# Registers from SBUF, one queue for the early weights, one table load and later mixes at the head of a conditional FFN kernel

## The chip, the cores and the metric

The kernel runs on one core of one Trainium2 chip. The metric is the device time of one execution in microseconds (us). Before the change the median of three runs is 1345.63 us (1345.31 to 1346.24). Differences of about 0.2%, some 2.7 us, are at the edge of what can be measured here.

## What is computed

The reference, cut to what matters:

```python
W = weights[condition]                       # (64, 64, 64), condition: 64 numbers from 0 to 15
y = einsum('bct,bcd->bdt', x, W)             # x as (64, 64, 1024)
y = y.reshape(4, 512, 1024)                  # read as the FFN's input
h = gelu(einsum('bsd,df->bsf', y, inter_w) + inter_b, approximate=True)   # F = 4096
out = x + einsum('bsf,fd->bsd', h, output_w) + output_b
```

x is (32, 64, 1024) in the inputs: 32 items with 64 channels and 1024 columns, so `condition` (called `cond` in the kernel) has 32 numbers that are used, and the result has the shape of x. All is float32. The first line matters most for this change: each item of x is multiplied by one of 16 matrices of 64 x 64, and which one is known only when the program runs.

## The kernel before

**Mixes.** Two items of x make a tile of 128 rows, so there are 16 tiles x_0 to x_15 (`NR` is 16). A *mix* (`mix`, from L299) multiplies one tile with a block-diagonal matrix of 128 x 128, `wsel(i)`, whose two blocks of 64 x 64 are the two items' matrices. It is eight matmuls into two PSUM tiles, and as float32 each is two instructions, 16 in all. The off-diagonal blocks are zeroed once by VectorE (`zero_wsel`). The diagonal blocks are fetched by `load_wsel` (from L263), two DMAs of 16 KB a tile, from `cond_w` at an address in a register; `load_indices` (from L251) reads eight such registers at a time, those of four tiles. The tiles 0 to 7 have their own blocks in `wsel_e`, the tiles 8 to 15 share two in `wsel_l` (`NL` is 8).

Mixes 0 to 7 (`mixed`, from L311) fill the first half of y in SBUF: ScalarE copies one PSUM tile, VectorE the other. Mixes 8 to 15 are for the second half: `load_later` brings tile and weights, `mixed_later` copies out, `store_later` writes to DRAM, where it is read again later. The order of the first eight is 0, 1, 2, 3, 6, 7, 4, 5.

**Products.** The two large products of the FFN are done by a scheme of Strassen's kind in two levels, 7 x 7 products of blocks where 8 x 8 would be needed. In its place come sums of blocks. POOL (GpSimd) makes those of the weights (`inner_w1`, `outer_w1`, through `pool_add`). VectorE and ScalarE make those of y and of the hidden values: `to_psum` copies one operand to PSUM (ScalarE, L202, tile t) and `add` sums on VectorE (L182). `right_sums` strings four such sums together. A product (`mm1`, L500) has eight instructions; it adds into one of the PSUM banks A, B and C, and `read` adds the bank into its target (fX, fD, ...) on VectorE, or copies it on ScalarE where the target is new (L475). w11, w12, w21 and w22 are the four blocks of the first piece of `inter_w`, 1 MB each.

**Order.** Every step is entered by hand with a due time, `at(time, fn, ...)`, and `run` sorts the steps by time and calls them. Times are in units of one product, 0 at the start of the first block; a block (`plan_block`) has seven products and begins every 7 units. Each engine does its instructions in that order, and waits in place for what they need. So do the two queues that issue DMAs: SP, which issues nearly all, and ScalarE, which issues some between its copies. The framework gives each DMA one of eight semaphores in turn, and an issue waits until the DMA before it on the same semaphore has landed.

**The head.** In the order of due times: `warm` (from L280) multiplies zeros, 11 times, while nothing has arrived; registers and weights of tiles 0 to 3 are read and issued on ScalarE, directly from `cond` in DRAM; the registers of tiles 4 to 7 are read on SP, also from DRAM, between the issue of x_1 and that of x_2; the weights of tiles 4 to 7 are issued on SP between the loads of x. `cond_s` is a copy of `cond` in SBUF, from which the later registers are read. Mixes 0, 1 and 2 come ahead of the first two products (fA, fB), then mixes 3, 6, 7, 4, 5, then the rest of block 0. Mixes 8 to 15 have the due times in `later` (L684). The first two of them use banks of the products, B and C; the others use the two PSUM buffers through which ScalarE's copies t also go (`pst`).

The activation table that ScalarE needs for a function is loaded ahead of the first instruction that needs another one than is loaded: before the change once ahead of the first copy and once ahead of the first gelu.

Of the kernel before, what the change touches and what calls it, by code (L numbers as in the profile page):

```python
# [9 lines left out]
F32 = mybir.dt.float32  # L10
AF = mybir.ActivationFunctionType
# [63 lines left out]
def kernel(  # L75
# [35 lines left out]
    nc = tc.nc  # L111
    P = 128
    B, C, T = x.shape
    S, _, D = cond_w.shape
    F = inter_w.shape[1]
    assert 2 * C == P and 2 * D == P
    NR = B // 2
# [31 lines left out]
    NL = 8  # L149
    b1 = const.tile([P, F // P], F32, name="b1")  # L150
    wsel_l = const.tile([P, 2, P], F32, name="wsel_l")
    cond_s = const.tile([1, B], cond.dtype, name="cond_s")
# [3 lines left out]
    misc = left1.enter_context(tc.tile_pool(name="misc", bufs=2))  # L156
# [16 lines left out]
    def at(time, fn, *args):  # L173
        steps.append((time, len(steps), fn, args))
# [30 lines left out]
    def right_sums(time, get, gap=0.5):  # L205


        e = {}
        v = nc.vector

        def one():
            e.update(get())
            e["p"] = to_psum(e["12"])

        def two():
            add(v, e["t3"], e["22"], e["p"], sub=True)

        def three():
            add(v, e["t1"], e["p"], e["11"], sub=True)
            e["p"] = to_psum(e["11"])  # L220

        def four():
            add(v, e["t2"], e["p"], e["t3"])
            e["p"] = to_psum(e["21"])

        def five():
            add(v, e["t4"], e["p"], e["t2"], sub=True)

        for j, f in enumerate((one, two, three, four, five)):
            at(time + j * gap, f)  # L230
# [11 lines left out]
    def wsel(i):  # L242
        return wsel_e[:, i, :] if i < NR - NL else wsel_l[:, i % 2, :]
# [7 lines left out]
    def load_indices(i0):  # L251


        eng = mybir.EngineType.SP if i0 else mybir.EngineType.Activation
        src = cond[None, :] if i0 < NR - NL else cond_s
        _, idx = nc.values_load_multi_w_load_instructions(
            src[:, 2 * i0 : 2 * i0 + 8], engines=[eng], min_val=0, max_val=S - 1,
            skip_runtime_bounds_check_because="the reference indexes cond_w by it",
        )
        for k, v in enumerate(idx):  # L260
            IDX[2 * i0 + k] = v

    def load_wsel(i):  # L263
        eng = nc.sync if i > 3 else nc.scalar
        for j in range(2):
            eng.dma_start(
                wsel(i)[j * C : (j + 1) * C, ts(j, D)],
                cond_w[bass.ds(IDX[2 * i + j], 1), :, :].rearrange("s c d -> (s c) d"),
            )
# [10 lines left out]
    def warm():  # L280


        z = misc.tile([P, 3 * P], F32, tag="m8", name="zeros")
        nc.vector.memset(z, 0.0)
        t = acc_pool.tile([P, 2, W], F32, tag="A", name="warm")
        for _ in range(11):
            nc.tensor.matmul(t[:, 1, :], z[:, :P], z[:, P:], start=True, stop=True)  # L287

    Y = {}
# [27 lines left out]
    def load_later(i):  # L317
        t = misc.tile([P, 2, T], F32, tag="m8", name=f"xl{i}")
        XT[i] = t[:, 0, :]
        YS[i] = t[:, 1, :].rearrange("p (k n) -> p k n", k=NK)  # L320
        nc.sync.dma_start(XT[i], x_rows[i])
        load_wsel(i)
# [50 lines left out]
    def inner_y(a, p):  # L373
        q = Y[a, RIGHT[p]]
        pool = yia if p in (1, 2) else late["yib"]
        t = lambda n: pool.tile([P, 2, W], F32, tag=f"yi{p}", name=f"y{n}_{a}_{p}")
        t1 = blk(q, 0, 1)
        if (a, p) == (0, 1):
            t1 = cpool.tile([P, 2, W], F32, tag="c", name="yi1_0_1")
        YI[a, p] = {  # L380
            "11": blk(q, 0, 0),
            "21": blk(q, 1, 0),
            "22": blk(q, 1, 1),
            "12": blk(q, 0, 1),
            "t1": t1,
            "t2": t("i2"),
            "t3": t("i3"),
            "t4": t("i4"),
        }
        return YI[a, p]  # L390
# [250 lines left out]


    at(-61, warm)
    order = FIRST
    at(-60.5, zero_wsel, wsel_e)
    at(-60, load_indices, 0)
    for i in range(4):
        at(-59, load_wsel, i)
    at(-50, load_indices, 4)
    for n in Y_ORDER:  # L650
        at(-45, new_y, 0, n)
    MIX = 1.06
    NB = 3
    t0 = 2 - (len(order) - NB) * MIX
    M_AT = {i: t0 + (j - NB) * MIX - (2 if j < NB else 0) for j, i in enumerate(order)}
    for j, i in enumerate(order):
        t = M_AT[i]
        if j < 6:
            at(-55 if j < 2 else -43 + 0.1 * j, load_x, i)
        else:  # L660
            at(M_AT[order[j - 6]] + MIX + 0.45, load_x, i)
        if i > 3:
            at(-43 + 0.1 * j, load_wsel, i)
        at(t, mix, i, None if j == 3 else "CB"[j % 2])
        at(t + MIX + 0.3, mixed, i)
    at(-54, lambda: nc.sync.dma_start(cond_s, cond[None, :]))
    t8 = M_AT[1] + MIX + 0.6
    at(-20, zero_wsel, wsel_l)
    at(t8, load_indices, 8)
    at(t8 + 0.5, load_indices, 12)  # L670
    at(-42.75, load_w1, 0, "11")
# [9 lines left out]
    right_sums(ty + 9.2, outer_y0(1, 0))  # L681
    for j, p in enumerate((6, 7, 4, 5, 3)):
        right_sums(7 * (j + 2) - (3.6 if p == 6 else 4.5), lambda p=p: inner_y(0, p))
    later = (4.02, 7.05, 12.5, 14.3, 21.8, 26.2, 33, 46.6)  # L684
    for j, t in enumerate(later):
        i = NR - NL + j
        at(max(t - 6, later[j - 2] + 3.3) if j > 1 else t8 + 0.4, load_later, i)
        at(t, mix, i, "BC"[j] if j < 2 else None)
        at(t + 1.4, mixed_later, i)
        at(t + 3.2, store_later, i)  # L690

# [8 lines left out]
    for it in range(nit):  # L700
# [5 lines left out]
        for n, t in W_AT.items():  # L706
            if it == 0:
                t = {1: -7.9, 2: -5.4, "s3": -4, "s1": -1}.get(n, t)
# [17 lines left out]
        if it == 1:  # L726
            for k in range(KQ):
                e = {}
                t = b0 + 5 + 10.8 * k
# [3 lines left out]
        elif it >= 2:  # L733
            n = -(-len(w2_pieces) // (nit - 2))
            for j in range(n):
                i = (it - 2) * n + j
                if i < len(w2_pieces):
                    e = {}
                    t = b0 + 9.5 + 14 * j
# [404 lines left out]
```

## Time and profile before

| what | value |
|---|---|
| median of three runs | 1345.63 us |
| the profiled execution: its own time | 1344.67 us |
| its span in the profile | 1342.7 us |
| TensorE (PE) busy | 1325.1 us, 99% |
| POOL, VectorE (DVE), ScalarE (ACT) busy | 945.6, 882.6, 486.5 us |
| mean granted TensorE clock | 0.999 |
| moved by DMA | 273.34 MB, mean 204 GB/s |

The span runs from the first to the last instruction that the profile records; the execution's own time is 2.0 us longer. Names like `py<-wsel_e,x` are the tile that is written and those that are read, with buffer numbers left out: `py` is a mix, `fA`, `fB` and `fC` are products by bank, `yi` and `yt` are sums of y, `wi` and `ws` sums of the weights, `xl` a late tile of x. "Idle before" is the time that an engine stood still ahead of an instruction, and behind the arrow stands what ended it.

Two things of the table can be misread. A busy PE is one that has an instruction in flight; at half clock it is as busy as at full. And the 70% of POOL and 66% of DVE are means over a kernel of several stages.

### The profile page before, as it was taken

How to read it: one execution, taken by the hardware profiler on the slowest of the kernel's cores; microseconds unless marked ns; L12 is line 12 of the kernel's file. 1: busy time of each engine (PE TensorE's matmuls, PEld its weight loads, DVE VectorE, ACT ScalarE, POOL GpSimd, SP SyncE). 2: the span in 40 equal slices, each digit the busy share in tenths (PEclk: the TensorE clock that was granted, in tenths of full speed). 3: DMA queues.
4: the chain of work that ended last, by engine and by line, in shares of the span. 5: the costliest groups of instructions: out<-in, count | busy, mean ns of one | idle time of the engine just before them, and what ended most of it. 6: DMA issues, size and time to landing. Idle time of an engine off the chain costs nothing.

```text
span 1342.7 us, 18524 instructions
## 1 busy us (share of the span) xinstructions
PE 1325.1 (99%) x6286; PEld 1163.0 (87%) x6286; DVE 882.6 (66%) x1573; ACT 486.5 (36%) x975; POOL 945.6 (70%) x583
## 2 busy tenths in 40 slices
PE   8899999999999999999999999999999999999998
PEld 7888888888888888888888888888888888888887
DVE  4667565575786765757658574675766757767776
ACT  3424324243353442534415332333324333333341
POOL 3754757948768396594962967949959599496793
PEclk9999999999999999999999999999999999999999
DMA  7656676777897866768749145183360723916712
GB/s 272 168 163 221 211 223 233 258 261 257 298 352 225 284 211 222 257 204 273 239 176 341 30 166 226 47 324 115 102 275 4 287 109 108 362 40 222 264 47 63
DMA packets 138176, 273.34 MB, mean 204 GB/s; under 512 B 17635, under 2 KB 71139, under 8 KB 126435
## 3 DMA queue, kind: packets, MB, share of 16 engines
q1 hardware_dynamic: 137170, 271.91, 58.8%
q8 instruction: 50, 0.82, 0.2%
q14 instruction: 44, 0.35, 0.1%
q10 hardware_dynamic: 912, 0.26, 0.1%
HBM read 167.27 MB, written 104.86 MB: 203 GB/s over the span
## 4 chain that ended last, share of the span: by engine, by line
PE 90%; DVE 4%; issue 2%; ACT 2%; POOL 1%; DMA 1%; SPq 0%; DVEq 0%; POOLq 0%; ACTq 0%
PE fA L500 26%; PE zA L511 24%; PE fC L500 12%; PE zC L511 12%; PE fB L500 7%; PE zB L511 6%; PE py L306 2%; DVE hs L182 1%; PE tp L998 1%; ACT t L202 1%; DMA wsel_l<-in_L_cond_weights_dram 1%; DVE fX L182 1%; POOL w2p L182 1%; PE warm L287 0%; DVE fV L182 0%
## 5 line engine op out<-in xcount | busy, mean ns | idle before, releaser
L500 PE MATMUL fA<-yi,wi 128*128 128x256 f32 x896 | 212.6, 380 | 3.3 <-DVE fX L182 1.5
L182 DVE TENSOR_TENSOR hs<-h,t 128x512 f32<-128x512 f32 x308 | 200.0, 679 | 5.6 <-ACT t L202 2.9
L511 PE MATMUL zA<-hs,wt 128*128 128x256 f32 x840 | 197.8, 379 | 0.0
L182 POOL TENSOR_TENSOR h<-h,h 128x1024 f32<-128x1024 f32 x84 | 196.1, 2364 | 0.0
L500 PEld LDWEIGHTS fA<-yi,wi 128*128 128x128 f32 x896 | 169.0, 190 | 29.8 <-issue 2.9
L511 PEld LDWEIGHTS zA<-hs,wt 128*128 128x128 f32 x840 | 158.5, 190 | 21.1
L182 POOL TENSOR_TENSOR wi<-w 128x512 f32<-128x512 f32 x80 | 101.7, 1272 | 53.0 <-PE fC L500 25.6
L525 ACT ACTIVATE fD<-fD,b 128x256 f32<-128x256 f32 x128 | 57.9, 500 | 186.2 <-DVE fD L182 181.7
L182 POOL TENSOR_TENSOR ws<-w,w 128x1024 f32<-128x1024 f32 x32 | 74.9, 2363 | 66.9 <-PE fA L500 47.5
L202 ACT COPY t<-h 128x512 f32<-128x512 f32 x140 | 81.8, 589 | 75.3 <-DVE hs L182 69.9
L202 ACT COPY t<-hs 128x512 f32<-128x512 f32 x112 | 65.4, 588 | 108.0 <-DVE hs L182 108.0
L182 POOL TENSOR_TENSOR wt<-v 128x512 f32<-128x512 f32 x35 | 44.6, 1274 | 82.5 <-DMA v<-w_d 70.2
L182 DVE TENSOR_TENSOR fX<-fA,fX 128x512 f32<-128x512 f32 x104 | 71.3, 685 | 44.4 <-PE fA L500 42.3
L182 POOL TENSOR_TENSOR wi<-w,wi 128x512 f32<-128x512 f32 x40 | 50.9, 1272 | 61.9 <-PE fA L500 48.7
L500 PE MATMUL fC<-y,wi 128*128 128x256 f32 x352 | 83.2, 379 | 0.1
L511 PE MATMUL zC<-hs,v 128*128 128x256 f32 x336 | 79.6, 379 | 0.8 <-DVE hs L182 0.8
L511 PE MATMUL zA<-h,wt 128*128 128x256 f32 x320 | 75.6, 379 | 0.0
L500 PE MATMUL fA<-yi,w 128*128 128x256 f32 x320 | 75.6, 379 | 0.0
L500 PEld LDWEIGHTS fC<-y,wi 128*128 128x128 f32 x352 | 66.7, 190 | 9.5 <-issue 0.5
L511 PEld LDWEIGHTS zC<-hs,v 128*128 128x128 f32 x336 | 63.6, 190 | 9.7 <-DVE hs L182 1.2
L500 PEld LDWEIGHTS fA<-yi,w 128*128 128x128 f32 x320 | 60.8, 190 | 8.3
L511 PEld LDWEIGHTS zA<-h,wt 128*128 128x128 f32 x320 | 60.6, 190 | 8.2
(181 smaller groups left out, 2778.1 us busy)
## 6 DMA issues: line engine op xcount, KB each, us to landing
h<-hs_d SPq DMA_DIRECT2D x56, 1024.0 KB, 5.3
w<-in_L_ffn_inter_w_dram SPq DMA_DIRECT2D x32, 1024.0 KB, 6.3
hs_d<-hs SPq DMA_DIRECT2D x96, 256.0 KB, 3.1
v<-w_d SPq DMA_DIRECT2D x21, 1024.0 KB, 9.8
hs_d<-fD SPq DMA_DIRECT2D x64, 256.0 KB, 3.4
w2p<-in_L_ffn_output_w_dram SPq DMA_DIRECT2D x32, 512.0 KB, 5.0
w_d<-w2p SPq DMA_DIRECT2D x64, 256.0 KB, 2.9
w_d<-w2t SPq DMA_DIRECT2D x48, 256.0 KB, 6.6
```

What stands on the lines that cost most here:

```text
L182: eng.tensor_tensor(o, a, b, ALU.subtract if sub else ALU.add)
L202: nc.scalar.copy(t, src)
L306: nc.tensor.matmul(PY[i][k // KQ][:, k % KQ, :], XT[i][:, ts(k, P)], wsel(i), start=True, stop=True,)
L500: nc.tensor.matmul(acc[:, u, :], lt[:, k, ts(u, P)], rt[:, k, :], start=start and u == 0 and k == 0, stop=k == 1, skip_group_check=True,)
L511: nc.tensor.matmul(acc, wl[:, k, :], hr[:, k, :], start=start and k == 0, stop=k == NG - 1, skip_group_check=True,)
L525: nc.scalar.activation(t[:, u, :], t[:, u, :], AF.Gelu_apprx_tanh, bias=b1[:, f : f + 1])
L998: nc.tensor.transpose(tp[:, v, ts(n0, P)], d[:, n0, ts(v, P)], late["ident"])
```

## The change

Six edits, all of them at the head:

- All registers are read from `cond_s` in SBUF, whose load becomes the first DMA that SP issues. Those of tiles 0 to 7 are read on ScalarE, the others on SP.
- ScalarE alone issues the weights of tiles 0 to 7. Those of 6, 7, 4 and 5 now stand behind the copies of mixes 0, 1 and 2.
- SP thereby has nothing to wait for between x_1, x_2 and w11.
- A gelu on one column of zeros is put ahead of everything on ScalarE, so that its table is loaded there. Copies need no table of their own behind it: the changed program has one table load, the old one two.
- Eight products of zeros instead of eleven.
- The late mixes 8 to 11 are due at 7.05, 11.03, 14.3 and 18.7 instead of 4.02, 7.05, 12.5 and 14.3. The first two change their banks. On TensorE that moves mix 8 behind three more products, mix 9 behind four, mix 10 behind two, mix 11 behind four; all else keeps its order.

```diff
     def load_indices(i0):
-        eng = mybir.EngineType.SP if i0 else mybir.EngineType.Activation
-        src = cond[None, :] if i0 < NR - NL else cond_s
+        eng = mybir.EngineType.SP if i0 >= NR - NL else mybir.EngineType.Activation
         _, idx = nc.values_load_multi_w_load_instructions(
-            src[:, 2 * i0 : 2 * i0 + 8], engines=[eng], min_val=0, max_val=S - 1,
+            cond_s[:, 2 * i0 : 2 * i0 + 8], engines=[eng], min_val=0, max_val=S - 1,
...
     def load_wsel(i):
-        eng = nc.sync if i > 3 else nc.scalar
+        eng = nc.sync if i >= NR - NL else nc.scalar
...
         t = acc_pool.tile([P, 2, W], F32, tag="A", name="warm")
-        for _ in range(11):
+        g = misc.tile([P, 1], F32, tag="m8", name="table")
+        nc.vector.memset(g, 0.0)
+        nc.scalar.activation(g, g, AF.Gelu_apprx_tanh)
+        for _ in range(8):
             nc.tensor.matmul(t[:, 1, :], z[:, :P], z[:, P:], start=True, stop=True)
...
     at(-60.5, zero_wsel, wsel_e)
+    at(-62, lambda: nc.sync.dma_start(cond_s, cond[None, :]))
     at(-60, load_indices, 0)
     for i in range(4):
         at(-59, load_wsel, i)
-    at(-50, load_indices, 4)
+    at(-58, load_indices, 4)
...
         if i > 3:
-            at(-43 + 0.1 * j, load_wsel, i)
+            at(M_AT[order[min(j - 4, 2)]] + MIX + 0.31, load_wsel, i)
...
-    at(-54, lambda: nc.sync.dma_start(cond_s, cond[None, :]))
...
-    later = (4.02, 7.05, 12.5, 14.3, 21.8, 26.2, 33, 46.6)
+    later = (7.05, 11.03, 14.3, 18.7, 21.8, 26.2, 33, 46.6)
     for j, t in enumerate(later):
...
-        at(t, mix, i, "BC"[j] if j < 2 else None)
+        at(t, mix, i, "CB"[j] if j < 2 else None)
```

## The prediction

> **What bounds the kernel now.** I read the page's busy line first, then PE's own waits, then the timeline and the clock of the stretch that the edits touch.
>
> ```profile
> span 1342.7 us, 18524 instructions
> ...
> PE 1325.1 (99%) x6286; PEld 1163.0 (87%) x6286; DVE 882.6 (66%) x1573; ACT 486.5 (36%) x975; POOL 945.6 (70%) x583
> ```
>
> PE bounds: only 17.6 us of the span is idle on it, and 8.8 of those lie in the first 90 us. PE's waits there (total, times, longest):
>
> ```profile
> PE py L306 <- DMA wsel_l<-in_L_cond_weights_dram: 4.0, 1, 4.0
> PE py L306 <- issue: 1.9, 1, 1.9
> PE py L306 <- DVE yi L182: 1.7, 1, 1.7
> PE warm L287 <- DVE zeros L284: 1.3, 1, 1.3
> ```
>
> All but the last stand in front of a mix (py; mix i works on x_i). The timeline places them (start, duration; ACTq and SPq are queues that issue DMAs):
>
> ```profile
> 4.51 5.17 ACTq L266 DMA_DIRECT2D wsel_e<-in_L_cond_weights_dram  x8
> 7.29 0.36 SPq L278 DMA_DIRECT2D x<-in_x_dram  x1
> ...
> 9.71 1.28 ACT L314 ACT_TABLE_LOAD   x1 [9.71 <-issue]
> ...
> 13.42 2.02 PE L306 MATMUL py<-wsel_e,x 128*128 128x128 f32 x16 [1.85 <-issue]
> ```
>
> Before 4.51 ACT reads its eight registers from cond in DRAM. SP does the same to 5.6 and then waits for the landing of wsel_e's second load at 7.28; only then may x_2 go. Mix 2 waits for its second half of weights, issued at 7.85 and landed 5.5 us later, 13.33. By start of instructions, mix 8 stands still from 31.22 to 35.38 (4.16) and mix 10 from 54.47 to 56.29 (1.82). The clock, in stretches (us, PE busy (count), granted clock, DMA share, GB/s):
>
> ```profile
> 35.38:38.86 3.48, 3.48 (x16) 0.51 0.93 16
> 56.29:58.18 1.89, 1.89 (x16) 1.00 0.69 269
> ```
>
> So mix 8 pays twice: its 16 instructions run at half clock and take 3.48 instead of the 16 x 0.111 = 1.78 of mixes 0 and 1.
>
> **Part by part.** Sums are against the profiled execution: 1344.67 us, of which 1342.7 is span and 2.0 lies around it. The runs' median, 1345.63, is 0.96 above; the forecast for a median adds that back.
>
> *Fewer zero products.* A product is two instructions. They start 0.43 apart until 4.81 and 0.216 apart from there. The six that go are among the later: 6 x 0.216 = 1.30. The last of 16 starts at 6.32, so mix 0 can start at 6.53 instead of 7.83, if its weights are there.
>
> *Registers from SBUF.* ACT's reads cost 0.88 + 2.71, SP's 2.51 + 0.92. From SBUF eight cost 0.53 to 0.71 (engine, instruction, count: ns min/median/max, first and last start).
>
> ```profile
> L256 SPq TENSOR_LOAD <-cond_s x2: 532/622/713, 22.8 to 28.6; - x2
> L256 ACTq TENSOR_LOAD <-in_itok_B_dram_ptr x1: 877/877/877, 0.7 to 0.7; - x1
> L256 ACTq TENSOR_LOAD <-in_itok_B_dram x1: 2712/2712/2712, 1.6 to 1.6; - x1
> L256 SPq TENSOR_LOAD <-in_itok_B_dram_ptr x1: 2512/2512/2512, 2.0 to 2.0; - x1
> ...
> L256 SPq TENSOR_LOAD <-in_itok_B_dram x1: 922/922/922, 4.7 to 4.7; - x1
> ```
>
> But now ACT waits for cond_s: issued at 0.74, landing about 2.0 later by the first wsel_e row below, 2.75. The read ends at 3.4, and the first wsel_e goes at 3.5 instead of 4.51, the second at 4.2. The table load (1.28 from 0.74, then a 1-column activation) ends by 2.4, inside that wait: cost nothing; if cond_s landed at once, up to 1.3.
>
> *SP is free early.* x_0, x_1, x_2 and w11 go from 1.1 to 2.4 instead of 0.74, 1.20, 7.29 and 7.71. So 2.5 MB are queued before the first wsel_e, and these rows (KB, issue to landing) decide the head:
>
> ```profile
> wsel_e<-in_L_cond_weights_dram ACTq DMA_DIRECT2D x4, 16.0 KB, 2.0
> ...
> wsel_e<-in_L_cond_weights_dram ACTq DMA_DIRECT2D x1, 16.0 KB, 6.4
> ```
>
> The four issued with little else under way took 2.0; those issued behind x_2, w11, x_3 and x_6 took 4.0, 5.5, 6.3 and 6.4. The last three landed 0.5 to 1.1 before the large load issued ahead of each did (w11 by POOL's first sum, 13.96). x_0 took 3.6 and x_1 came 1.25 after it, so x_0, x_1, x_2, w11 land at 4.7, 5.95, 7.2 and 9.7. I take 0.5 before w11: both halves for mix 0 at 9.2. Bounds: 6.53 (nothing in the way) and 4.2 + 6.4 = 10.6.
>
> Then mix 0 runs at 9.25, mix 1 at 11.0, mix 2 at 12.8, and the first product fA at 9.25 + 3 x 1.78 = 14.6 instead of 15.28: **-0.7**, from -3.4 (9.25 becomes 6.53, fA 11.9) to +2.3 (10.6, and mix 0 at half clock).
>
> The new list of waits ties queues together, since eight DMA semaphores go round and an issue waits until the one before on its semaphore has landed (before, SP stood 2.6 us so):
>
> ```profile
> SPq L278 <- DMA wsel_e<-in_L_cond_weights_dram: 2.6, 2, 1.7
> ```
>
> x_3 waits for mix 0's weights, x_6 for w11, x_7 for mix 1's. On ACT the copies of mixes 0 to 2 alternate with wsel_e 6, 7, 4, 5, at 0.65 a piece (5.17 / 8), and the last four of these wait for x_3, x_6 and x_7. By x_2's 3.7 and 1.3 more for each following, these land at 12.9, 14.2 and 15.5. The last wsel_e is out at 16.8, and the copy of fA runs to 17.4. Mix 7 needs the bank behind it and starts at 14.6 + 2 x 1.73 + 2 x 1.78 = 21.6 (1.73 for a product of eight instructions), so 3 us cover the ACT work. Without that cover each later microsecond of x_7 costs one.
>
> *First late mix three products later, loads earlier.* w12 waits for mix 7's first weights, which go out behind mix 1's copy at 12.9 and, with x_2's 3.7, land at 16.6; so w12 goes then instead of at 21.08, and w21, w22, x_8 and wsel_l go behind it. Before, wsel_l landed 35.24 - 21.08 = 14.2 after w12's issue; that gives 31, and mix 8 now starts at 14.6 + 2 x 1.73 + 5 x 1.78 + 5 x 1.73 = 35.6. The wait and the half clock go: -4.16 - 1.70 = **-5.86**. What is late next is POOL's sums for the second block. They start with w12's landing (28.1 before, about 21 now) and move as far as PE does.
>
> *Table load out of 49.69, mix 10 behind two more products.* Mix 10's wait hangs on a chain of t copies on ACT and yi sums on DVE, which that load of 1.28 holds up. DVE also loses its 5.8 us behind mix 8 and starts the dense part early. -1.82 - 0.11 (its first instruction) = **-1.93**; bounds: 0 and this.
>
> *Mix 11, four products later.* Its second bank needs the yi sum that ended 8.15 us after fB began (70.89 + 0.68 against 63.42). In the new order that bank is due after 4 x 1.73 + 0.89 = 7.8: **+0.4**, between 0 and the 1.93 of mix 10.
>
> Sum: -0.7 - 5.86 - 1.93 + 0.4 = -8.1. After mix 11 PE's order is the same, and PE stays the bound. Profiled 1336.6, **median 1337.5**.
>
> [...]
>
> **Rivals.**
> - *The small loads overtake.* Mix 0 starts at 6.53 and fA at 11.9: another 2.7, **1334.8**. For it: 16 KB took 2.0 when alone. Against: the four rows. 0.22.
> - *The head goes cold.* PE idles from 6.5 to 9.2, 2.7 us. A pause of 2.1 (11.3 to 13.42) left the clock up, one of 4.16 halved it. If 2.7 does, mix 0 costs 1.70 more: **1339.2**. 0.13.
> - *Late mixes still wait for sums.* They take both banks in which ACT puts its copies; one or two more waits like mix 10's give **1339.4 or 1341.4**. 0.12.
> - *Slower.* All of mixes 10 to 15 wait so, because PE no longer gives DVE and ACT the pause of mix 8. Place: py L306 behind yi L182. Price: 1.93 each, six in place of one, with the head and mix 8 gained: -0.7 - 5.86 + 5 x 1.93 = +3.1, **1348.7**; it turns slower from the fourth added wait. Against: DVE is 66% busy, and only one of six waited. 0.03.
> - *Nothing comes of it.* The wait moves to another late load, say x_10, whose issue follows the stores of mix 8: within 0.2%. Against: mix 8's last store goes at 38.1 and lands 2.8 later, x_10 and its weights are issued by 43.4 and landed by 46 to 48, and mix 10 is due at 51.3. 0.05.
>
> **How the numbers follow.** My case, 1337.5, has 0.45; the rest are above and sum to one. 0.2% is 2.7 us, about what a measurement of this kernel can tell from no change. Faster by more: 0.45 + 0.22 + 0.13 + 0.10 = 0.90; within: 0.05 + 0.02 = 0.07 (three waits of the third rival among them); slower: 0.03. The range 1334.0 to 1341.5 takes in both ends of the head (-11.2 and -5.1 in all), the cold head and two more waits.
>
> **What would show it.** Right: the first wsel_e issued at 3.5 and landed with w11; fA at 14.6; no PE wait at mix 8 and a granted clock of 1.00 there; one table load; a short wait at mix 11 alone. Wrong: mix 0 at 6.5; half clock in the first mix; py waiting behind yi more than once; SP's w12 later than 18, or x_7 landing after 18, which would put ACT's copy of fA in front of mix 7.

## The result and the profile after

| | before | after |
|---|---|---|
| median of five runs | 1345.63 us (1344.54 to 1346.24) | **1338.06 us** (1337.19 to 1338.83) |
| the profiled execution: its own time, its span | 1344.67, 1342.7 us | 1337.99, 1336.0 us |
| ratio of after to before, 95% interval | | 0.9945, 0.9933 to 0.9956 |

The kernel became 0.55% faster. The forecast of 1337.5 is 0.56 us below the median, and the range held it. The page of after, its span and its busy line:

```profile
span 1336.0 us, 18508 instructions
...
PE 1322.4 (99%) x6280; PEld 1160.3 (87%) x6280; DVE 882.8 (66%) x1574; ACT 485.4 (36%) x975; POOL 946.3 (71%) x583
```

PE's busy time fell by 2.7 us and its idle time from 17.6 to 13.6. The first is mostly the half clock of mix 8, in which PE had counted as busy (1.70), and the zero products, busy for 5.62 instead of 6.67. All waits of PE in the first 90 us (total, times, longest):

```profile
PE py L309 <- DMA wsel_e<-in_L_cond_weights_dram: 3.4, 1, 3.4
PE warm L290 <- DVE table L287: 1.3, 1, 1.3
```

The three waits at mixes 8, 2 and 10 are gone, and a new one of 3.4 stands at mix 0. The timeline gives the places (start, duration, in brackets the idle time before):

```profile
1.33 5.62 PE L290 MATMUL warm<-zeros 128*128 128x256 f32 x16 [1.33 <-DVE table L287]
10.37 5.59 PE L309 MATMUL py<-wsel_e,x 128*128 128x128 f32 x48 [3.43 <-DMA wsel_e<-in_L_cond_weights_dram]
15.81 1.89 PE L503 MATMUL fA<-y,w 128*128 128x256 f32 x8
36.83 1.95 PE L309 MATMUL py<-wsel_l,xl 128*128 128x128 f32 x16
52.49 1.95 PE L309 MATMUL py<-wsel_l,xl 128*128 128x128 f32 x16
61.33 2.37 PE L309 MATMUL py<-wsel_l,xl 128*128 128x128 f32 x16
```

The rows are mix 0 (with 1 and 2), the first product, and mixes 8, 10 and 11. Mixes 8 and 10 start without a wait. Mix 11 takes 2.37 where the others take 1.95. The clock of two stretches (us, PE busy (count), granted clock, DMA share, GB/s):

```profile
10.37:12.20 1.83, 1.83 (x16) 1.00 0.39 89
36.83:38.60 1.77, 1.77 (x17) 1.00 0.00 0
```

Mix 0 and mix 8 both run at a granted clock of 1.00. So the gain is where the forecast put it, and the head, which was to start 0.7 earlier, starts 0.53 later in this execution.

### The profile page after: what moved, and what is told of

The parts are those of the page before. It is cut to its first block, busy times and chain, and to the rows that moved or that the text cites. A ratio compares the mean times of both kernels' runs of the same rounds, so it can differ in the third digit from the quotient of the medians.

```text
span 1336.0 us, 18508 instructions
## 1 busy us (share of the span) xinstructions
PE 1322.4 (99%) x6280; PEld 1160.3 (87%) x6280; DVE 882.8 (66%) x1574; ACT 485.4 (36%) x975; POOL 946.3 (71%) x583
## 4 chain that ended last, share of the span: by engine, by line
PE 91%; DVE 4%; POOL 1%; issue 1%; ACT 1%; DMA 1%; ACTq 0%; DVEq 0%; POOLq 0%
PE fA L503 26%; PE zA L514 24%; PE fC L503 12%; PE zC L514 12%; PE fB L503 7%; PE zB L514 6%; PE py L309 2%; DVE hs L182 1%; PE tp L1002 1%; POOL w2p L182 1%; DVE fX L182 1%; ACT t L202 1%; DVE fV L182 0%; DMA hs_d<-hs 0%; DVE mZ L182 0%
## 5 line engine op out<-in xcount | busy, mean ns | idle before, releaser
L182 POOL TENSOR_TENSOR wt<-v,wt 128x512 f32<-128x512 f32 x35 | 44.6, 1274 | 32.9 <-PE zA L514 28.6
```

What stands on the lines that cost most here:

```text
L182: eng.tensor_tensor(o, a, b, ALU.subtract if sub else ALU.add)
```

## The experiments

Each kernel was timed five times, run 3 eleven times, beside the kernel before on the same chip. Ratios are to that kernel, whose median was 1344.88 us beside runs 1, 2, 5 and 6, 1345.25 beside runs 3, 7, 8 and 9, and 1344.45 beside runs 4 and 10. The theory was that moving the late mixes brings nearly all, and that the head brings nothing because small loads land in the order in which they were issued among the large ones. The rivals were that the earlier loads or the table load bring the gain, and that ScalarE's small loads go their own way.

### 1. The late mixes alone

```diff
 # the kernel before
-    later = (4.02, 7.05, 12.5, 14.3, 21.8, 26.2, 33, 46.6)
+    later = (7.05, 11.03, 14.3, 18.7, 21.8, 26.2, 33, 46.6)
-        at(t, mix, i, "BC"[j] if j < 2 else None)
+        at(t, mix, i, "CB"[j] if j < 2 else None)
```

> The kernel before with the new due times and banks of the late mixes alone; head, registers, queues and tables as before. My theory (the gain is the place of the late mixes): mix 8 is due at 31.22 + 3 x 1.73 = 36.4, its weights land at 35.2 as before, so its 4.16 us of waiting and 1.70 of half clock go; mix 10's 1.93 goes too, mix 11 costs 0.6. So 7 us under before, 1338.4, as fast as the changed kernel. Rival (the gain is the earlier loads): the weights of mix 8 are still too late, some 2 us under before, 1343.5.

Measured: 1337.47 us, ratio 0.9948 (0.9934 to 0.9961). PE's waits, complete as above:

```profile
PE warm L287 <- DVE zeros L284: 1.3, 1, 1.3
PE py L306 <- issue: 0.4, 1, 0.4
PE py L306 <- ACT t L202: 0.3, 1, 0.3
```

Neither `wsel_l` nor `yi` is left among them. Mix 8 starts at 36.50 and mix 10 at 52.16, both without a wait. Mix 8's weights land at 35.35, no earlier than before (35.24), so the gain does not need the earlier loads. The old table load is still there:

```profile
L525 ACT ACT_TABLE_LOAD  x1: 1283/1283/1283, 42.1 to 42.1; - x1
```

Two lines of the change bring 7.41 us. The other five edits, which the whole change adds to them, bring nothing that can be measured (0.9945 against 0.9948).

### 2. All but the late mixes

```diff
 # the kernel after
-    later = (7.05, 11.03, 14.3, 18.7, 21.8, 26.2, 33, 46.6)
+    later = (4.02, 7.05, 12.5, 14.3, 21.8, 26.2, 33, 46.6)
-        at(t, mix, i, "CB"[j] if j < 2 else None)
+        at(t, mix, i, "BC"[j] if j < 2 else None)
```

> The changed kernel with the old due times and banks of the late mixes. Theory: mix 8 is due at 31.65 and its weights land at 33.81, as they do in the changed kernel: a wait of 2.2 at full clock in place of 5.86; mix 10 waits 0 to 1.8 again. With the head's +0.5 that is 3 to 5 us under before: 1340.5 to 1342.5. Rival (the earlier loads make the gain): the late weights are there, and the time is that of the changed kernel, 1338.

Measured: 1339.96 us, ratio 0.9960 (0.9946 to 0.9973). PE's waits and the clock of mix 8:

```profile
PE py L309 <- DMA wsel_l<-in_L_cond_weights_dram: 3.2, 1, 3.2
PE py L309 <- DMA wsel_e<-in_L_cond_weights_dram: 2.5, 1, 2.5
PE warm L290 <- DVE table L287: 1.3, 1, 1.3
PE py L309 <- DVE yi L182: 0.8, 1, 0.8
```

```profile
34.27:36.29 2.02, 2.02 (x17) 1.00 0.09 6
```

In their old places, mix 8 waits 3.15 instead of 3.99 (the idle time of PE by the profile; the 4.16 of the prediction counts by starts) and keeps a clock of 1.00, and mix 10 waits 0.8 instead of 1.7. The median is 0.5 below the range that was expected; the profiled execution, 1341.10, is the slowest of the five and lies in it. So the other edits are worth 4.92 us by themselves and the move 7.41, but together 7.57: for the most part both remove the same waits. That is why a gain measured with one edit alone must not be added to another's. Of the five other edits only the table load was run by itself (run 3); which of the rest brings the loads forward is open.

### 3. The table load alone

```diff
 # the kernel before, warm
         t = acc_pool.tile([P, 2, W], F32, tag="A", name="warm")
+        g = misc.tile([P, 1], F32, tag="m8", name="table")
+        nc.vector.memset(g, 0.0)
+        nc.scalar.activation(g, g, AF.Gelu_apprx_tanh)
         for _ in range(11):
```

> The kernel before with the one-column gelu put ahead of everything on ACT, so that one table load is left, at the start. Theory: the load of 1.28 at 49.69 was part of mix 10's wait, which falls from 1.82 to the 0.8 that it has in the run with the old mixes; mix 8 waits as before. About 1 us under before. Rival: mix 10 waits for DVE, which lost its time behind mix 8, and the table load cost nothing: no change, below what the runs can tell.

Measured: 1343.59 us, ratio 0.9983 (0.9974 to 0.9992). PE's waits, and the clock of mix 8:

```profile
PE py L309 <- DMA wsel_e<-in_L_cond_weights_dram: 2.8, 2, 1.5
PE py L309 <- DMA wsel_l<-in_L_cond_weights_dram: 2.7, 1, 2.7
PE warm L290 <- DVE table L287: 1.3, 1, 1.3
PE py L309 <- DVE yi L182: 0.8, 1, 0.8
```

```profile
35.83:39.17 3.34, 3.34 (x17) 0.57 0.89 12
```

Here the head is worse by 1.84 (fA at 17.12). With the edit x_2 was issued at 5.71 instead of 7.29, beside the second half of mix 0's weights (5.63), which landed at 9.56, 0.21 behind x_2, instead of 7.28. In the same way the second half of mix 1's weights was issued at 6.92, beside w11 (6.84), and landed at 13.09 instead of 8.54. Yet the kernel is faster, by 1.66 in the median; its profiled execution is the slowest of the eleven, with a span only 0.3 shorter than before. Mix 8's wait shrank from 3.99 to 2.71, so 1.28 of the head's 1.84 fell into it. Mix 10's wait shrank from 1.7 to 0.8. This is the key to the kernel before: most of what its head lost had no price, since mix 8 waited for its weights anyway.

### 4. Eleven products of zeros

```diff
 # the kernel after
-        for _ in range(8):
+        for _ in range(11):
```

> The changed kernel with eleven products of zeros, as before. Theory: mix 0 waits for its weights until 10.2 in any case, and the six instructions end before, at 8 to 8.6; no change, 1338. Rival (the zeros were on the path, as my sum had it): 1.3 slower.

Measured: 1337.10 us, ratio 0.9944 (0.9930 to 0.9958), the ratio of after. The zeros end at 8.17 and mix 0 starts at 9.54, so they were not on the path. This kernel's head is after's in all else, and fA starts at 14.97; in run 2, also with this head, at 15.11. So the profiled executions of this head spread by 0.84 us.

### 5. The first weights on SP, in the order of need

```diff
 # the kernel after
-        eng = mybir.EngineType.SP if i0 >= NR - NL else mybir.EngineType.Activation
+        eng = mybir.EngineType.Activation if i0 == 4 else mybir.EngineType.SP
...
-        eng = nc.sync if i >= NR - NL else nc.scalar
+        eng = nc.sync if i < 4 or i >= NR - NL else nc.scalar
...
-    at(-60, load_indices, 0)
-    for i in range(4):
-        at(-59, load_wsel, i)
+    at(-54.5, load_indices, 0)
+    for i, t in enumerate((-54.4, -54.3, -42.78, -42.69)):
+        at(t, load_wsel, i)
```

SP then issues x_0, x_1, the weights of 0 and 1, x_2, those of 2, w11, x_3, those of 3.

> The changed kernel, but SP itself reads the registers of tiles 0 to 3 and issues their weights in the order of need: x_0, x_1, weights 0 and 1, x_2, weights 2, w11, x_3, weights 3. Theory (the first weights are late because 2.5 MB stand ahead of them in the DMA engines): mix 0 starts at 6.6 instead of 10.37, the first product at 12.0 instead of 15.81, and all of it lasts: 1334.3. Rival (sums on DVE, ACT or POOL or the next loads limit what follows): the head gains 3.8 but waits further on give it back, 1337 to 1338.

Measured: 1337.45 us, ratio 0.9942 (0.9929 to 0.9956). Mix 0's weights land at 6.41 and 6.62 and mix 0 starts at 7.89, 2.5 earlier than in after. But SP took some 0.65 for each small issue (in before four of them start 0.65 to 0.67 apart, from 15.56 to 17.53), so w11 goes at 7.70 and lands at 14.39:

```profile
PE warm L290 <- DVE table L287: 1.3, 1, 1.3
PE fA L503 <- DMA w<-in_L_ffn_inter_w_dram: 1.1, 1, 1.1
PE py L309 <- ACT t L202: 0.5, 1, 0.5
PE py L309 <- issue: 0.4, 1, 0.4
```

The first product waits 1.1 for w11, mix 3 0.4 at its issue and mix 6 0.5 for a copy of ScalarE. The third product fC starts at 28.36 (28.19 in after): the head's gain is given back before it ends, as the rival had it.

### 6. SP reads the late registers between x_0 and x_1

```diff
 # the kernel after
-            at(-55 if j < 2 else -43 + 0.1 * j, load_x, i)
+            at(-55 if j < 1 else -54 if j < 2 else -43 + 0.1 * j, load_x, i)
...
-    at(t8, load_indices, 8)
-    at(t8 + 0.5, load_indices, 12)
+    at(-54.5, load_indices, 8)
+    at(-54.4, load_indices, 12)
```

The two register reads hold x_1 back to 3.36, between the two halves of mix 0's weights (2.92 and 3.67). x_2 and w11 follow only at 7.21 and 7.58: x_2 then waits 3.5 for the landing of mix 0's second half, which has the semaphore before it. No load changes its queue.

> The changed kernel, but SP reads the late registers between x_0 and x_1, so that x_1, x_2 and w11 go after 3.3 us; the first weights still go from ACT at 2.9 and 3.7. Theory (a small load waits for what was issued ahead of it on either queue): the first half of mix 0's weights lands at about 5, the second at 6.5, mix 0 starts at 6.6; 1334.5. Rival (large loads of SP go first, whatever the order of issue): both halves land behind x_1 and x_2, after 8, 1336.

Measured: **1336.16 us** (1335.99 to 1336.43), ratio 0.9935 (0.9921 to 0.9948). The second half of mix 0's weights (KB, issue to landing), first in after, then here:

```profile
wsel_e<-in_L_cond_weights_dram ACTq DMA_DIRECT2D x1, 16.0 KB, 6.6
```

```profile
wsel_e<-in_L_cond_weights_dram ACTq DMA_DIRECT2D x1, 16.0 KB, 3.5
```

Issued at 3.68 and 3.67, with the same instruction on the same queue, it takes 6.6 behind x_0, x_1, x_2 and w11, and 3.5 behind x_0 and x_1, landing at 7.19, 0.21 behind x_1. The first half, issued 0.44 ahead of x_1, lands at 5.98, 1.00 ahead of it. Thus ScalarE's small loads did not overtake the x loads that SP had issued ahead of them; the same load took 6.6 or 3.5 with what stood in front of it when it was issued. Mix 0 starts at 7.36 without a wait, fA at 13.97, 1.84 earlier than in after and 1.33 earlier than the mean of after, run 2 and run 4, now with 0.6 for w11. The span is 1.8 shorter than after's: since mix 8 no longer waits, what the head gains comes out at the end. The time is the rival's 1336 and not the theory's 1334.5, but not for the rival's reason, since neither half came after 8. Mix 0 started 0.8 later than the theory said, and w11 and mix 2 cost 0.8 more.

### 7. w11 behind x_3

```diff
 # the kernel after
-    at(-42.75, load_w1, 0, "11")
+    at(-42.65, load_w1, 0, "11")
```

> The changed kernel with w11 issued behind x_3 and not ahead of it; by its semaphore it then waits for x_1. Theory (the small loads get through only when the large load beside them ends): beside x_3, half as large, the second half of mix 0's weights lands at 9.5 instead of 10.24; w11 lands at about 12.5, the first product starts at 14.8, 1.0 earlier, 1337.0. Rival (what they run beside does not matter): mix 0 at 10.3 and the changed kernel's time, 1338.

Measured: 1336.95 us, ratio 0.9939 (0.9926 to 0.9953). The second half of mix 0's weights lands at 9.30, w11 at 12.18 and fA starts at 14.87, as the theory had it. But runs 2 and 4, with w11 ahead of x_3, had landings of 9.54 and 9.40 and fA at 15.11 and 14.97. That is too near to tell, and the run is inconclusive on what w11 alone costs the small loads.

### 8. Tile 0's registers and weights on SP, the rest on ScalarE

```diff
 # the kernel after; load_pair reads two registers on SP, those of one tile
+    def load_pair(i):
+        _, idx = nc.values_load_multi_w_load_instructions(
+            cond_s[:, 2 * i : 2 * i + 2], engines=[mybir.EngineType.SP], min_val=0,
...
-        eng = nc.sync if i >= NR - NL else nc.scalar
+        eng = nc.sync if i == 0 or i >= NR - NL else nc.scalar
...
-    for i in range(4):
-        at(-59, load_wsel, i)
+    at(-54.5, load_pair, 0)
+    at(-54.4, load_wsel, 0)
+    for i in range(1, 4):
+        at(-59, load_wsel, i)
```

> The changed kernel, but SP reads the two registers of tile 0 behind x_0 and x_1, issues its two weight loads, then x_2 and w11; ACT issues those of tiles 1 to 7 as before. Theory: mix 0's weights land at 6.5, mix 1's at 8, mix 2's by 10.5, w11, which waits for a semaphore, at 12.5; the first product at 12.6 instead of 15.8 and all of it lasts: 1334.9. Rival (the next loads give it back, as in the run with all first weights on SP): a wait at w11 or in mixes 3 to 5, 1336 to 1337.

Measured: 1336.38 us (1335.32 to 1339.30), ratio 0.9941 (0.9927 to 0.9955). Four small loads, two of each queue, land between 6.37 and 6.87, behind x_1's 6.20 at one spacing of 0.17, whichever queue they are of. Mix 0 starts at 7.01, but w11, issued behind them on SP at 6.39, lands at 13.57 and fA waits 1.1 for it, as the rival had it:

```profile
PE warm L298 <- DVE table L295: 1.3, 1, 1.3
PE fA L511 <- DMA w<-in_L_ffn_inter_w_dram: 1.1, 1, 1.1
PE py L317 <- DMA wsel_e<-in_L_cond_weights_dram: 0.2, 1, 0.2
```

In this execution the wait goes from mix 0 to fA, and part of the gain with it.

### 9. Run 8 with mix 11 one product later

```diff
 # run 8
-    later = (7.05, 11.03, 14.3, 18.7, 21.8, 26.2, 33, 46.6)
+    later = (7.05, 11.03, 14.3, 19.7, 21.8, 26.2, 33, 46.6)
```

> As e8_split, with mix 11 due at 19.7 instead of 18.7, one product later. Theory: the 0.58 that mix 11 loses waiting for banks of the yi sums go: 0.6 under e8_split. Rival: the wait moves to the product or the mix behind it: the same time as e8_split.

Measured: 1336.27 us (1335.49 to 1339.64), ratio 0.9940 (0.9927 to 0.9954). The 0.58 that mix 11 costs in after is gone, and mix 12, which now comes sooner behind it, waits 0.87:

```profile
60.08 1.95 PE L317 MATMUL py<-wsel_l,xl 128*128 128x128 f32 x16
66.34 2.05 PE L317 MATMUL py<-wsel_l,xl 128*128 128x128 f32 x16 [0.87 <-ACT xl L336]
```

The wait was moved, not removed. The head is run 8's, but here w11 lands at 12.53 and fA starts at 12.97 without a wait, so run 8's 1.1 is not a fixed price of this order.

### 10. Run 6 with mixes 11 and 12 later

```diff
 # run 6
-    later = (7.05, 11.03, 14.3, 18.7, 21.8, 26.2, 33, 46.6)
+    later = (7.05, 11.03, 14.3, 19.7, 22.3, 26.2, 33, 46.6)
```

> As e6_registers_between, with mixes 11 and 12 due at 19.7 and 22.3 instead of 18.7 and 21.8, one product later each. Theory: mix 11's 0.58 goes and mix 12, two products further from it than in e9_split_mix11, does not take over the wait of 0.87 that stood there: 0.6 under e6_registers_between. Rival: the two banks of the copies stay the limit and a wait of the same size stands at mix 12 or 13: the same time.

Measured: **1335.81 us** (1335.65 to 1336.21), ratio 0.9935 (0.9921 to 0.9948). Mixes 11 and 12 start without a wait:

```profile
61.30 1.95 PE L309 MATMUL py<-wsel_l,xl 128*128 128x128 f32 x16
68.27 1.95 PE L309 MATMUL py<-wsel_l,xl 128*128 128x128 f32 x16
```

Behind mix 12, fC starts at 70.06 instead of run 6's 70.47. This is the lowest median of all, 0.65% below the kernel before; run 6, on another chip, has the same ratio. Beside run 4, which is after with three more zero products and ran on the same chip, it is 1.29 us faster, and the two sets of five runs do not overlap. By run 6 most of that is the head; by the two traces mixes 11 and 12 are worth 0.4 of the 0.6 expected, which the times alone could not show.

## Why the prediction was right, and where it was not

The terms of the sum, from the profiled execution of before to that of after:

| step | predicted | measured | from |
|---|---|---|---|
| head, start of fA | -0.7 | +0.53 | 15.28 to 15.81 |
| mix 8, wait and half clock | -5.86 | -5.86 | no wait, clock 1.00 |
| mix 10 | -1.93 | -1.93 | no wait |
| mix 11 | +0.4 | +0.58 | fA to fC 4.09; 3.51 without a mix's delay |
| sum | -8.1 | -6.68 | own time 1344.67 to 1337.99 |

The four terms add up to the difference to the hundredth by chance: beside them mixes 3 to 5 took 0.09 less, and what follows mix 12 some 0.1 more.

- **The late mixes: right, and shown.** Run 1 has this alone and gets the whole gain. Mix 8 was due at 36.83 (predicted 35.6), and its weights landed at 33.81 (predicted 31), so the cover was 3.0 instead of 4.6. In run 2 the due time is about 31 and the wait is back. Mix 11 waits for what the prediction named: its second half starts at 62.57, behind the yi sum that ends at 62.42.
- **Mix 10: the size right, the cause half right.** The prediction gave the table load and the two added products together. Run 3 and run 2 show that the early table leaves 0.8 of 1.7 in the old place; run 1 shows that the place does without the early table. In run 1 the load also comes earlier, at 42.1 instead of 49.69, some 10 us ahead of mix 10.
- **The head: the term that failed.** It took the landing of mix 0's two halves at 9.2, "0.5 before w11", w11 at 9.7 and x_2 at 7.2. They came at 8.33 and 10.24, 11.25 and 8.13. In after, the weights' first packet moved only at 6.94, 0.40 after w11's first at 6.54. Three small loads landed while w11 moved, at 8.33, 10.24 and 10.94, 1.3 apart on average (0.8 in runs 2 and 4). The prediction let w11 move as if alone, 2.5 us behind x_2, and the small loads take no time at all. Measured was 3.1 (3.2 in runs 2 and 4); later w21 and w22, with no small load beside them, came 2.69 and 2.77 behind the load before them, so w11's own pace is part of that. Three profiled executions with this head put fA at 15.81, 15.11 and 14.97, on average 15.30. The kernel before had 15.28, and its head in run 1 14.97. So the new head gains nothing that shows, and part of the +0.53 is spread: x_2 landed at 7.32 and 7.41 in runs 2 and 4, near the predicted 7.2, and mix 0's second half at 9.54 and 9.40, not far behind the 9.2. The bound of 10.6 held.
- **Fewer zero products: hidden, as said on condition.** The prediction let mix 0 start at 6.53 "if its weights are there". They were not, and run 4 shows no price for the three products.
- **ScalarE's and SP's chain: later than said, without harm.** w12 went at 19.55 (predicted 16.6), since the first of mix 7's weights landed only at 19.54; x_7 was there only by 17.86 (15.5), when the issue that waited for it went; ScalarE's copy of fA ended at 20.39 (17.4). Mix 7 began at 22.8, so 2.4 of cover remained. The prediction had named 18 for w12 as a sign of a wait there. It was passed by 1.55 and nothing waited: the limit was drawn too tight.
- **cond_s** was there by 1.99, when ScalarE's read of it began, not at 2.75. The first weights went at 2.92, not 3.5. That lead was lost again in the queue.
- **The median came nearer than the sum.** The profiled time was forecast at 1336.6 and measured at 1337.99. The prediction added 0.96 for the distance of before's execution to its median; after's lies 0.07 from its own. Without that the forecast of the median would have been 1.5 low. That it is 0.56 low is in part luck.

Of the rivals, the small loads did not overtake: mix 0 at 10.37, not 6.53, and in runs 6 and 8 they landed right behind the x loads issued ahead of them (0.21 and 0.17), on either queue. They passed in part only the large load that was issued last before them: w11 in after (8.33, 10.24 and 10.94, ahead of its 11.25), and in run 7 x_3, 0.34 ahead of which the first half landed. At a near tie the start of an issue did not decide: the first of the prediction's four slow loads was issued at 7.20, not behind x_2 but 0.09 ahead of it, and the one of run 3 0.08 ahead, yet both landed 0.2 behind x_2. Their issues ended 0.04 later than x_2's. x_1 and x_2 were not passed in after: the first landing, 8.33, is behind x_2's 8.13. While w11 moved, from 7.0 to 9.5, ScalarE's queue moved 275 packets beside 440 of SP's; what let the small loads pass w11, no run here separates. The head did not go cold, although the pause was 3.43 and not 2.7: the clock of mix 0 was 1.00. Late mixes waited for sums once, at mix 11, for 0.58.

## What to carry to other kernels

A wait in the middle of a critical engine can absorb gains and losses ahead of it, and did here: remove it first, so that work on the head comes out at the end (in run 3 mix 8's wait took in 1.28 of the 1.84 that the head lost; in run 6 the head started 1.84 earlier than in after, and the span was 1.8 shorter). In after the queue that no longer waited issued four large loads ahead of the second half of mix 0's weights, which took 6.6, and in run 6 two, and it took 3.5: see to it that what is needed first is also issued first. In run 6, holding SP back, x_1 by two register reads and x_2 by a semaphore, was worth more than freeing it (ratio 0.9935 against 0.9945). Edits that remove the same wait do not add (4.92 and 7.41 gave 7.57), so each is to be measured on top of the others.

## What the runs showed of the hardware

- **The clock after a pause.** Idle times of 3.43 (after) and 3.15 (run 2) ahead of a mix left the granted clock at 1.00. One of 3.99 (before) halved it (0.51 over mix 8), and in run 3 one of only 2.71 did: there the first three instructions still ran at full speed, and the slow ones, with a clock of 0.51, began 0.4 us after the pause. So in these runs the length of the pause alone did not decide: one of 2.71 halved the clock and one of 3.43 did not. What else entered, no run here shows.
- **The slow start is of changing length.** The instructions of the zero products started 0.43 us apart at first and 0.216 apart later, and the change came after about 7 of them in run 10 and 14 in run 5. So the same 16 took from 5.17 us (run 10) to 6.73 (run 5), the same 22 from 6.67 (before) to 7.79 (run 1). That moves mix 0 where it is the zeros that it follows (in before it starts at 7.83, the last of the zeros at 7.62). The early spacing is twice the later one, as the 0.213 of mix 8 in before, at a clock of 0.51, is about twice the 0.111 of mixes 0 and 1; but the granted clock in the profile reads 1.00 there too (before, 1.3 to 4.8).
- **Small loads.** Loads of 16 KB landed 0.17 apart behind x_1 in run 8 and 0.17 to 0.19 apart behind w11 in after (four between 11.60 and 12.15), and 0.5 to 1.9 apart while w11 moved (after, runs 2 and 4).
- **Shared semaphores.** In after x_3 was held to 10.26 by the landing of mix 0's weights at 10.24 and w12 to 19.55 by that of mix 7's at 19.54, neither of which they use. The DMAs in the trace of after carry eight semaphore numbers, 81 or 82 DMAs each, and x_3 and w12 carry those of these two loads: here a small load that landed late delayed a large one on another queue.
